# An AdaLN block with a routed FFN on one core: scatters of two sequences read their slot list directly instead of through copied columns

## The chip, the cores and the metric

The kernel runs on one core of a Trainium2 chip. The metric is the time of one execution on the device, in microseconds (us), as the median of several runs. Engines are called as in the profile: PE is TensorE's matmuls, PEld its weight loads, DVE is VectorE, ACT is ScalarE, POOL is GpSimd, and SP is the engine whose queue issues most plain DMAs here. Times inside an execution are those of one profiled execution, counted from the start of its span.

## The reference, cut to what matters

Four sequences of 512 tokens with 128 features pass through one AdaLN block: a convolutional branch, then a mixture of 160 small experts of which each token uses eight, and a shared expert. Both branches are modulated by six vectors per sequence, computed from a condition `c`.

```python
mod = silu(c) @ wmod                              # (4, 6 * 128): sa, ca, ga, sb, cb, gb
ga, gb = sign(ga) * max(|ga|, 0.25), ...          # gates, kept away from zero
h = layernorm(x) * (1 + ca) + sa
# conv branch: rmsnorm, linear 128 -> 512, gate and value,
# two depthwise convolutions, linears, gate, linear 256 -> 128, plus h
x = x + ga * conv_branch(h)
h = layernorm(x) * (1 + cb) + sb                  # called h2 in the kernel
# routed FFN over all 4 * 512 tokens
probs = sigmoid(h @ router_w.T + bias)            # 160 experts
top_w, top_idx = top_k(probs, 8)
top_w = 2.5 * top_w / (sum(top_w) + 1e-9)
h1 = silu(einsum('th,eih->eti', h, w_gate))       # 128 -> 64 for each expert
routed = einsum('eti,ehi->th', h1 * combine.T, w_down)
shared = silu(h @ w_gate_shared.T) @ w_down_shared.T
x = x + gb * (routed + shared)
```

All data are float32. The reference computes every expert for every token; the kernel computes only the chosen ones.

## The kernel before, in words

**Tiles.** A sequence `b` (0 to 3) lies on chip as 128 partitions x 4 token tiles x 128 features. Its work is a generator, `sequence(b)` (lines 286 to 588), which is advanced in stages so that the stages of neighbouring sequences interleave. It computes the modulation, the conv branch (projections L328, convolution taps on PE L370 and on DVE L375), adds `x` (L405), then the second norm and `h2`. Half of `h2` is made by DVE and the other half, two token tiles, by two steps on POOL (a multiplication at L456, an addition at L457). Router probabilities and their top eight follow (DVE, L444 and around), then the ranks of each token within its expert, and at L517 `slot_in`, a list of 4 x 8 unsigned integers per partition: for token tile `t` and choice `k`, the row of a DRAM table in which that token's `h2` is to be put. Near its end the generator runs the shared expert; `wdg` (L569, DVE) and `hs` (L571, ACT) belong to it.

**Scatter.** `dispatch(b)` (lines 632 to 674) puts the 512 rows of `h2` into the table, eight times each. That is 32 indirect DMAs of 128 rows, issued by POOL at L666, each with one column `slot_in[:, t, k]` as its list of rows. Sequences 0 and 1 go into table 0, sequences 2 and 3 into table 1. Some of the scatters do not read the column from `slot_in`; a POOL copy (L664) brings the column into another tile, `pick`, first, and the scatter reads `pick`. In `dispatch(0)` and `dispatch(1)` a copy is made for those 26 of the 32 scatters for which there is no other step to be put in between; the six others have, ahead of them, one of six residual steps (`residual_sums(b + 2)`, L594, L595, L596: `h * gate + x + bias` of sequence `b + 2`, two token tiles at a time), and read `slot_in`. In `dispatch(2)` and `dispatch(3)` every scatter has its copy, and the steps in between are weights of earlier sequences (`places`, L620) and additions of the shared expert's output (L650).

**Experts.** `experts(s)` (lines 681 to 775) works through table `s` in groups of eight blocks. A group loads its rows (`xg`, SP, L690), transposes them on PE (L696), copies them out of PSUM (`xs`, L697, by DVE for s = 0 and by ACT for s = 1), multiplies by the gate weights (L722), applies silu on ACT (L730), multiplies by the down weights (L735) and stores the rows into a result table (ACT's queue, L709). Ten groups have fixed weights; seven more are overflow blocks, for experts with more rows than one block holds. Their weights `ow` are loaded by SP with an address from a register (L749, eight loads a group, two buffers) and used at L759 and L769.

**Combine.** `combine(b)` (lines 778 to 818) fetches, for each token tile and choice, the 128 result rows by an indirect DMA on POOL (L809), 32 for each sequence. For sequences 0 and 1 POOL also multiplies each fetched block by its weight (L786) and DVE adds (L795); for 2 and 3 DVE does both (L791, L793). Sequences 0 and 1 read result 0, sequences 2 and 3 result 1. After the last fetches come the gate and the final addition (L797, L798), and SP stores the output (L985).

**What sets the order.** The main part (lines 961 to 986) emits the stages of the sequences with `dispatch(b - 1)` after them, then `experts(0)`, `combine(0)`, `combine(1)`, `experts(1)`, `combine(2)`, `combine(3)`. That is the order of emission only. A scheduler then decides, when the kernel is built, in which order each engine issues its instructions, from its own estimates of their durations; `behind(b, what)` is a hint to it that an instruction is not to be issued ahead of another. So a removed instruction can also move others. On the chip the order on each engine is fixed, and the engines wait for one another through semaphores.

Some tiles share a buffer by their tag, so that the later one waits until the earlier is read for the last time: `pick` uses the tag of `keys`; `bits` of `places` (L606) that of the modulation `mod` of the sequence two later, which the POOL steps of `h2` read last; `wdg` of sequence 3 (L569) that of `out_bg` of sequence 3, which the last residual step L596 reads; `hs` of sequence 2 (ACT) that of the input `u_f` of the POOL steps of `h2` of sequence 2.

A dense fallback for lists that do not fit (lines 987 on) is guarded by a flag and is not taken with these inputs.

Of the kernel before, what the change touches and what calls it, by code (L numbers as in the profile page):

```python
# [92 lines left out]
def adaln_block(  # L93
# [22 lines left out]
    def own(b, shape, dtype, tag, name):  # L116
        return work.tile(shape, dtype, tag=f"{tag}{b % 2}", name=f"{name}_{b}", bufs=1)
# [165 lines left out]
    def behind(b, what):  # L283
        return tc.issue_after(last[what, b].ins) if (what, b) in last else nullcontext()
# [305 lines left out]
    def residual_sums(b):  # L590
        h, x, mod, out_bg = residual[b]
        for i in range(2):
            at = ds(2 * i, 2)
            yield nc.gpsimd.tensor_mul(h[:, at, :], h[:, at, :], wide(mod[:, 2, :])[:, at, :])  # L594
            yield nc.gpsimd.tensor_add(h[:, at, :], h[:, at, :], x[:, at, :])  # L595
            yield nc.gpsimd.tensor_add(h[:, at, :], h[:, at, :], wide(out_bg)[:, at, :])  # L596
# [35 lines left out]
    def dispatch(b):  # L632


        h2, slot_in = scattered[b]
        pick = own(b, [P, NT, TOPK], U32, "keys", "pick")

        def steps():
            if b < 2:
                for _ in range(11):  # L640
                    yield None
                yield from residual_sums(b + 2)
            else:
                for _ in range(4):
                    yield None
                for other in ((0,), (1, 2))[b - 2]:
                    yield from places(other, nc.gpsimd)
                x1 = x_sb[b]
                for t in range(NT):
                    yield nc.gpsimd.tensor_add(x1[:, t, :], x1[:, t, :], shared[b][:, t, :])  # L650

        between = steps()
        for t in range(NT):
            for k in range(TOPK):
                i = t * TOPK + k
                step = None
                if i and (b >= 2 or i % 2 == 0 or i < 12):
                    with behind(b, "scatter"):
                        step = next(between, None)
                at = slot_in[:, t, k : k + 1]  # L660
                if step is None or b >= 2:
                    at = pick[:, t, k : k + 1]
                    with behind(b, "scatter"):
                        nc.gpsimd.tensor_copy(at, slot_in[:, t, k : k + 1])  # L664
                with behind(b, "scatter") if i else behind(b - 1, "scatter"):
                    last["scatter", b] = nc.gpsimd.indirect_dma_start(  # L666
                        out=tables[b // 2], out_offset=bass.IndirectOffsetOnAxis(ap=at, axis=0),
                        in_=h2[:, t, :], in_offset=None, bounds_check=ROWS - 1, oob_is_err=False,
                    )
                ins = last["scatter", b].ins  # L670
                tc.declare_no_dep(ins, group=f"dispatch{b // 2}", reason="different rows")
                tc.add_to_no_dep_group(f"dispatch{b // 2}", ins)
        for _ in between:
            pass
# [286 lines left out]
    for b in range(B):  # L961
        if 0 < b < 2:
            next(parts[b])
        next(parts[b])
        if b:
            next(parts[b - 1])
        if b == 1:
            with behind(0, "kept"):
                w_pairs = [weights(g) for g in range(NGO - 2)]
        next(parts[b])  # L970
        if 0 < b < B - 1:
            next(parts[b + 1])
        if b:
            dispatch(b - 1)
    next(parts[B - 1])
    dispatch(B - 1)
    for _ in places(B - 1, nc.vector):
        pass
# [79 lines left out]
```

## Time and profile before

| | before |
|---|---|
| three runs | 506.87, 509.65, 512.99 us; median 509.65 |
| profiled execution | 505.33 us, span 503.6 us |
| granted TensorE clock, mean | 0.804 of full speed |
| idle POOL ahead of scatters of `dispatch` (page, group L666) | 34.2 us |
| HBM traffic | 50.54 MB read, 47.45 MB written |

By stage of the span, busy time of each engine in us:

| stretch, us | what runs | PE | DVE | ACT | POOL | clock | DMA share |
|---|---|---|---|---|---|---|---|
| 65 to 121 | scatters of sequence 0 | 49.72 | 42.86 | 25.04 | 46.50 | 0.88 | 0.47 |
| 121 to 177 | scatters of sequence 1 | 36.14 | 31.75 | 18.84 | 47.09 | 0.81 | 0.27 |
| 177 to 299 | experts(0); scatters of 2 and 3 | 91.31 | 55.40 | 37.47 | 83.71 | 0.85 | 0.66 |
| 299 to 411 | experts(1); combine(0), combine(1) | 76.76 | 20.81 | 56.43 | 87.73 | 0.88 | 0.75 |
| 411 to 504 | combine(2), combine(3) | 0.00 | 29.19 | 0.00 | 63.26 | 0.50 | 0.20 |

The clock is the share of full TensorE speed that was granted, and the DMA share is the mean busy share of the core's 16 DMA engines. A POOL instruction that issues an indirect DMA is counted as busy while POOL works on it; the transfer itself goes on after it. A busy share in a table like this says nothing yet on what an engine waits for; that is read from timelines, where each line gives start, duration, engine, source line and operation, and in brackets the idle time before it with what ended it.

### The profile page before, as it was taken

What the parts mean: (1) busy time and instruction counts of PE and PEld (TensorE: products, weight loads), DVE (VectorE), ACT (ScalarE), POOL (GpSimd) and SP (SyncE); (2) the same over time, 40 slices, a digit from 0 to 9 for tenths busy, and PEclk for the clock granted to TensorE, in tenths of its full rate; (3) what the DMA queues carried; (4) which work ended last, traced back from release to release, by engine and by line L of the source; (5) the groups of instructions that cost most, each with busy time, mean ns of one, the idle gap of its engine ahead of it and who ended that gap; (6) DMA issues with size and microseconds to landing.
All of it is one profiled execution on the core that took longest, in us unless ns stands there. A gap on an engine that the chain in (4) does not pass through costs nothing.

```text
span 503.6 us, 6524 instructions
## 1 busy us (share of the span) xinstructions
PE 305.3 (61%) x1892; PEld 223.2 (44%) x1892; DVE 225.5 (45%) x712; ACT 170.7 (34%) x358; POOL 359.7 (71%) x520
## 2 busy tenths in 40 slices
PE   4896996897749659768586665775877910000000
PEld 2654443444323349767575564665766900000000
DVE  7387785795595336574362220201223204333331
ACT  3563636343704227222232131643666610000000
POOL 7716168887888878748877507888889838777771
PEclk9799998699669959889798785995999875555555
DMA  8999996016410246558698566565999832122111
GB/s 262 409 385 409 362 423 259 31 57 179 142 36 32 89 169 205 180 195 278 198 327 267 182 204 209 190 191 181 309 325 348 293 113 63 52 52 73 52 53 38
DMA packets 50364, 98.50 MB, mean 196 GB/s; under 512 B 7633, under 2 KB 26130, under 8 KB 48914
## 3 DMA queue, kind: packets, MB, share of 16 engines
q1 hardware_dynamic: 36144, 61.20, 35.8%
q0 software_dynamic: 8192, 16.79, 11.2%
q10 hardware_dynamic: 5986, 20.03, 10.2%
q8 instruction: 17, 0.28, 0.2%
q14 instruction: 25, 0.20, 0.1%
HBM read 50.54 MB, written 47.45 MB: 195 GB/s over the span
## 4 chain that ended last, share of the span: by engine, by line
PE 37%; POOL 21%; issue 17%; DVE 9%; DMA 8%; ACT 4%; another core or an unknown queue 1%; SPq 1%; ACTq 0%; POOLq 0%; DVEq 0%
POOL yk L809 10%; PE ph L722 7%; POOL table L666 6%; PE py L735 6%; PE px L696 5%; DMA xg<-table 4%; PE pc L370 4%; PE py L769 3%; PE ph L328 3%; PE ph L759 2%; POOL dia L918 1%; DMA result<-yg 1%; PE py L392 1%; DMA ow<-in_w_ov 1%; DMA yk<-result,row 1%
## 5 line engine op out<-in xcount | busy, mean ns | idle before, releaser
L809 POOL DMA_INDIRECT yk<-result,row x128 | 125.2, 978 | 56.1 <-issue 37.0
L666 POOL DMA_INDIRECT table<-h,pick x116 | 118.8, 1024 | 34.2 <-POOL pick L664 17.3
L696 PE MATMUL px<-ident,xg 128*128 128x128 f32 x272 | 43.4, 297 | 26.0 <-DMA xg<-table 22.6
L735 PE MATMUL py<-w_g,h_own 128*128 128x128 f32 x320 | 45.4, 295 | 14.6 <-issue 7.7
L735 PEld LDWEIGHTS py<-w_g,h_own 128*128 128x128 f32 x320 | 41.6, 207 | 16.9 <-ACT h_own L730 8.5
L722 PE MATMUL ph<-xs,w_g 128*128 128x128 f32 x320 | 47.4, 307 | 0.3 <-DVE xs L697 0.3
L696 PEld LDWEIGHTS px<-ident,xg 128*128 128x128 f32 x272 | 33.0, 151 | 31.2 <-DMA xg<-table 22.0
L722 PEld LDWEIGHTS ph<-xs,w_g 128*128 128x128 f32 x320 | 43.9, 219 | 2.7 <-issue 0.7
L793 DVE SCALAR_TENSOR_TENSOR out_sb<-yk,idx,out_sb 128x128 f32<-128x128 f32 x56 | 20.3, 362 | 49.9 <-DMA yk<-result,row 47.2
L697 DVE COPY xs<-px 128x512 f32<-128x512 f32 x34 | 22.8, 685 | 42.9 <-remote 12.4
L795 DVE TENSOR_TENSOR out_sb<-out_sb,yk 128x128 f32<-128x128 f32 x48 | 15.0, 321 | 58.0 <-POOL yk L786 33.7
L730 ACT ACTIVATE h_own<-ph 64x256 f32<-64x256 f32 x80 | 30.3, 379 | 26.3 <-PE px L696 10.2
L707 ACT COPY yg<-py 128x512 f32<-128x512 f32 x34 | 19.9, 586 | 56.4 <-PE px L696 19.3
L664 POOL COPY pick<-slot_in 128x1 uint32<-128x1 uint32 x116 | 25.6, 222 | 17.0 <-DVE slot_in L517 16.5
L769 PE MATMUL py<-ow,h 64*128 64x128 f32 x224 | 19.6, 317 | 22.6 <-issue 15.6
L769 PEld LDWEIGHTS py<-ow,h 64*128 64x128 f32 x224 | 16.6, 216 | 26.6 <-issue 18.0
L370 PE MATMUL pc<-val,dia 128*128 128x512 f32 x64 | 28.1, 592 | 0.0
L786 POOL TENSOR_TENSOR yk<-yk,idx 128x128 f32<-128x128 f32 x64 | 25.8, 412 | 1.0
L375 DVE SCALAR_TENSOR_TENSOR s<-val,vec,s 128x512 f32<-128x512 f32 x32 | 24.9, 778 | 0.6
L697 ACT COPY xs<-px 128x512 f32<-128x512 f32 x34 | 19.3, 588 | 14.9 <-issue 11.8
L328 PE MATMUL ph<-hf,in_wn 128*128 128x512 f32 x32 | 21.3, 806 | 0.8 <-issue 0.7
L708 DVE COPY yg<-py 128x512 f32<-128x512 f32 x17 | 11.7, 687 | 19.2 <-issue 7.9
(249 smaller groups left out, 551.4 us busy)
## 6 DMA issues: line engine op xcount, KB each, us to landing
table<-early SPq DMA_DIRECT2D x2, 8704.0 KB
xg<-table SPq DMA_DIRECT2D x34, 512.0 KB
result<-yg ACTq DMA_DIRECT2D x34, 512.0 KB
ow<-in_w_ov SPq DMA_DIRECT2D x112, 96.0 KB
w_g<-in_w_gd SPq DMA_DIRECT2D x10, 1024.0 KB
yk<-result,row POOLq DMA_INDIRECT x128
table<-h,pick POOLq DMA_INDIRECT x116
x<-in_x SPq DMA_DIRECT2D x4, 256.0 KB
```

Source lines behind the costliest of these rows:

```text
L328: nc.tensor.matmul(ph, in_wn[:, ts(o, P)], hf, start=True, stop=True)
L370: nc.tensor.matmul(pc, dia[:, k, :], val[:, 0, k : k + L], start=(k == 0), stop=(k == npe - 1))
L664: nc.gpsimd.tensor_copy(at, slot_in[:, t, k : k + 1])
L666: last["scatter", b] = nc.gpsimd.indirect_dma_start(out=tables[b // 2], out_offset=bass.IndirectOffsetOnAxis(ap=at, axis=0), in_=h2[:, t, ...
L696: nc.tensor.transpose(px[:, c, :], xg[:, 4 * half + c, :], ident)
L697: (nc.scalar.copy if s else nc.vector.tensor_copy)(xs[:, ds(4 * half, 4), :], px)
L722: nc.tensor.matmul(ph[:, c, :, :].rearrange("u r (i q) -> u r i q", i=8), w[:, j, 0, :], xs[:, :, ds(16 * j, 16)].rearrange("f i (r q) -> ...
L730: nc.scalar.activation(h4[at, :, mine, :], ph4[at, :, mine, :], AF.Silu)
L735: nc.tensor.matmul(py[j & 1][:, j // 2, :], h, w[:, j, 1, :], start=True, stop=True)
L769: nc.tensor.matmul(py[r][:, c, :], h[at, c, :], ow[at, c, r, ds(r * INTER, D)], start=True, stop=True)
L786: last["weight", b] = nc.gpsimd.tensor_mul(row, row, wk[:, t, k : k + 1].to_broadcast([P, D]))
L809: last["fetch", b] = nc.gpsimd.indirect_dma_start(out=yk[:, k, :], out_offset=None, in_=results[b // 2], in_offset=bass.IndirectOffsetOnAx ...
```

## The change

In `dispatch`, the condition under which a column is copied loses its first half. `dispatch(0)` and `dispatch(1)` copy no columns any more, and all of their 64 scatters read `slot_in`; `dispatch(2)` and `dispatch(3)` are as before. 52 POOL instructions fall away. The tile `pick` is still declared for every sequence. Nothing else is edited; the line numbers behind the edit grow by one, because of a blank line. The scheduler orders the changed program anew.

```diff
@@ dispatch(b)
                     with behind(b, "scatter"):
                         step = next(between, None)
                 at = slot_in[:, t, k : k + 1]
-                if step is None or b >= 2:
+                if b >= 2:
                     at = pick[:, t, k : k + 1]
                     with behind(b, "scatter"):
                         nc.gpsimd.tensor_copy(at, slot_in[:, t, k : k + 1])
```

## The prediction

> **What bounds the kernel now.** I read the page's engine table and costliest groups, then the chain of work that ended last, then the timelines of GpSimd (POOL), VectorE (DVE), TensorE (PE) and the SP queue at the places where that chain changes engine, and last the built instruction order of the changed kernel beside the old one. The profiled execution took 505.33 us with a span of 503.6; the median of the three runs is 509.65 (506.87 to 512.99). I sum against the span and add 509.65 - 503.6 = 6.05 at the end.
>
> Engines and groups of the page:
> ```profile
> PE 305.3 (61%) x1892; PEld 223.2 (44%) x1892; DVE 225.5 (45%) x712; ACT 170.7 (34%) x358; POOL 359.7 (71%) x520
> L809 POOL DMA_INDIRECT yk<-result,row x128 | 125.2, 978 | 56.1 <-issue 37.0
> L666 POOL DMA_INDIRECT table<-h,pick x116 | 118.8, 1024 | 34.2 <-POOL pick L664 17.3
> L664 POOL COPY pick<-slot_in 128x1 uint32<-128x1 uint32 x116 | 25.6, 222 | 17.0 <-DVE slot_in L517 16.5
> ```
> POOL is busiest, and nearly all of it is 128 scatters and 128 fetches of about 1 us each. But it is not one chain. The chain that ended last runs on POOL from 138 to 197 us (scatters), on PE from 202 to 404 us (the experts), and on POOL again from 411 to 484 us (fetches). So the change, which touches the scatters at 65 to 176 us, has to pass through two hand-overs before it reaches the end.
>
> The price of a copy, timeline of POOL (start, duration, engine, line; idle before in brackets):
> ```profile
> 118.54 0.98 POOL L666 DMA_INDIRECT table<-h,pick  x1 [0.28 <-issue]
> 119.52 0.19 POOL L664 COPY pick<-slot_in 128x1 uint32<-128x1 uint32 x1
> 119.99 0.98 POOL L666 DMA_INDIRECT table<-h,pick  x1 [0.28 <-issue]
> 121.28 0.97 POOL L666 DMA_INDIRECT table<-h,pick  x1 [0.31 <-issue]
> ```
> With a copy between, scatters start 1.45 us apart; without one 1.29 us apart. The copy's 0.19 us mostly replaces idle time.
>
> First hand-over, POOL to DVE and PE. POOL's last residual step of sequence 3, its last scatter into the first table, and the last step of h2 of sequence 3:
> ```profile
> 159.10 0.74 POOL L596 TENSOR_TENSOR h<-h,out_bg 128x256 f32<-128x256 f32 x1
> 175.05 0.98 POOL L666 DMA_INDIRECT table<-h,pick  x1 [0.28 <-POOL pick L664]
> 196.11 0.72 POOL L457 TENSOR_TENSOR h<-u_f,mod 128x256 f32<-128x256 f32 x1
> ```
> and who waits for them:
> ```profile
> 159.88 0.28 DVE L569 TENSOR_TENSOR wdg<-wds,gb_tok 64x128 f32<-64x128 f32 x1 [5.39 <-POOL h L596]
> 182.76 0.69 DVE L697 COPY xs<-px 128x512 f32<-128x512 f32 x1 [9.33 <-issue]
> 196.86 0.18 DVE L606 TENSOR_SCALAR bits<-row 128x32 uint32<-128x32 uint32 x1 [1.69 <-POOL h L457]
> ```
> ```profile
> 181.60 3.02 PE L696 MATMUL px<-ident,xg 128*128 128x128 f32 x12 [8.91 <-DMA xg<-table]
> ```
> DVE stood 5.39 us for the residual (its buffer goes to wdg of sequence 3), DVE and PE some 9 us for the first table, and DVE 1.69 us for h2 of sequence 3 (its modulation buffer becomes bits of places(1)). Behind that last wait stand DVE's top-8 steps of sequence 3, and behind those PE.
>
> Second hand-over, the start of experts(1), timelines of PE and of the SP queue:
> ```profile
> 297.46 1.16 PE L769 MATMUL py<-ow,h 64*128 64x128 f32 x16 [0.86 <-ACT h L764]
> 308.02 2.91 PE L696 MATMUL px<-ident,xg 128*128 128x128 f32 x12 [9.40 <-DMA xg<-table]
> 310.72 2.99 PE L722 MATMUL ph<-xs,w_g 128*128 128x128 f32 x16
> 313.54 1.13 PE L696 MATMUL px<-ident,xg 128*128 128x128 f32 x8
> ```
> ```profile
> 289.74 13.37 SPq L749 DMA_DIRECT2D ow<-in_w_ov  x16
> 303.21 0.84 SPq L690 DMA_DIRECT2D xg<-table  x2
> ```
> PE idles 9.40 us because SP issues both sets of overflow weights ahead of the first table load, and the second set waits for PE's last matmul of experts(0).
>
> Third, POOL waits for the second result table at the first fetch that reads it:
> ```profile
> 401.74 0.98 POOL L809 DMA_INDIRECT yk<-result,row  x1 [0.16 <-issue]
> 403.31 1.02 POOL L809 DMA_INDIRECT yk<-result,row  x1 [0.16 <-issue]
> 410.98 0.95 POOL L809 DMA_INDIRECT yk<-result,row  x1 [6.64 <-issue]
> ```
> It arrives at 404.6 and stands until 410.98. From there to the end of the span nothing waits but POOL's own queue: 92.6 us. So the end is the time at which that fetch may start, plus all that stands behind it on POOL.
>
> **The change, part by part.** Removed: 52 copies (26 in each of dispatch(0) and dispatch(1); the other 12 scatters read the list already). Nothing is added. The copies were also what the scheduler wove other work around, so its order changes, and three moves matter.
>
> 1. Copies. 52 x 0.166 (1.456 - 1.29) = 8.6 us of POOL. Bounds: nothing, if the scatter itself sets the 1.46 pace in a long row; 0.47 each (copy plus the 0.28 idle behind it), 24 us, if all of it goes. The trace has several bare pairs at 1.29, so I take 0.166. The later 64 fetches without anything between them run at 1.25, so a long bare row is possible on this queue.
>
> 2. Order on POOL before 200 us. The scatters of sequences 0 and 1 now stand as 30, then two residual steps, then 2; the other residual steps follow. Before the last scatter into table 0 four residual steps and one h2 step (0.75 each) are gone too: 8.6 + 3.8 = 12.4, so its end moves from 176.0 to about 163.5. But the last residual step of sequence 3 now stands behind it: five steps of 0.77 and a copy, ready at about 167.5 instead of 159.84. The h2 step of sequence 2 also moves there (146.8 to about 165.7), and ScalarE's hs of sequence 2, which reuses its input buffer, waits with it (154.22 before) with the four copies of low behind it. DVE's wait for the residual grows by 7.7, less one conv tap (0.75) that now stands ahead of it, or 6 to 7. Sequence 3's addition of x, 172.73 before, comes at about 178.7. PE's first transpose of table 0 then starts at once, near 178.7 instead of 181.60: of the 9 us stall, 3 are won, 6 went into a new wait.
>
> Then that lead meets the h2 step of sequence 3. In the old order 11 scatters of sequence 2 stand ahead of its end, in the new order 19. POOL: -8.6 + 8 x 1.456 + one more addition (0.5) = +3.5, or about 200.3 instead of 196.83. Counting the steps one by one with the grouped residual steps at 0.77 gives 199.3. I take +3. DVE, 2.9 early, waits there about 6 us more than before, and everything behind runs 3 us late. The first experts are covered by PE's own work from there; I let the 3 us pass through: experts(0) ends at 301.6 instead of 298.6, and the first fetch of combine starts at 306.7 instead of 303.67. Of SP's queue: the first table loads are issued 12 us earlier, which now costs and brings nothing more than the above. slot_in of sequence 3 comes 3 us late, but POOL stood 4.38 us for it before and still does; its scatters end near 288 instead of 284.9, before table 1 is wanted at 297.
>
> 3. Order on SP at experts(1). The first two loads of table 1 now stand ahead of the second set of overflow weights. First set: issue from 289.74 + 3, 8 of the 16 loads in 4.5 us, so the table load goes at 297.2 and lands 4.77 us later (303.21 to 307.98 before), at 302.1: PE starts 5.9 us earlier than 308.02. The idle shrinks from 9.4 to under 1 us, and the slow matmuls after it go (granted clock 0.5 in that slice): 12 transposes in 2.91 and 16 matmuls in 2.99, against 8 in 1.04 and 16 in 1.95 a little later, 1.3 + 1.0 = 2.4 us. Result 1 may be read at 410.98 - 5.9 - 2.4 = 402.7. Bounds: nothing of the 8.3 (it comes back as waits for later loads, of which the old chain has 4.40 at 332 and 5.93 at 384), all of it.
>
> 4. Order on POOL at the end. The first fetch from result 1 now stands behind 59 fetches and 53 weightings instead of 64 and 58. Fetch and weighting together take 1.57 to 1.61 (401.74 to 403.31; 398.51 to 400.13), so five pairs, 8.05 us, that were done ahead of the wait now stand behind it. POOL arrives at 306.7 + 92.6 = 399.3 and waits until 402.7. The end: 402.7 + 92.6 + 8.05 = 503.4, against 503.6: nothing. With the 6.05 it is 509.4.
>
> A rule that speaks against the change: the Trainium skill, SBUF — State Buffer, "A bandwidth-pool intuition that's wrong", says that GpSimd can't write descriptors while DVE holds the shared port, and gives about 620 ns alone and 3100 ns beside a DVE copy. By it, an estimate, 64 bare scatters beside a busy DVE would cost up to 2.5 us more each, 160 us. The trace decides: beside a DVE that is busy 42.9 of the 56 us from 65 to 121, scatters mostly take 0.98 and the longest of all 1.69, so I add nothing.
>
> **The rivals.** *Slower, by the queue position.* The 8.3 us of move 3 don't reach result 1, because loads and weights of the later groups wait instead. Then result 1 comes at 410.98 + 3 = 414.0 and the end at 414.0 + 92.6 + 8.05 = 514.6, run 520.7. Half of the gain lost gives 507.5, run 513.6. For it: experts(1) has table-load waits right up to 390. Against: their sum is set by PE's release of buffers, which moves with PE. It decides from result 1 at 408 us on (more than 1% slower).
>
> *Faster.* The 3 us of move 2 are absorbed (PE has gaps of 1 to 5 us between 207 and 282 that wait for nothing the profile shows, and a late PE may run into them), and result 1 comes before POOL does. Then only POOL counts: 303.67 + 92.6 + 92.6 + 8.05 = 496.9, run 503.0. For it: POOL would have no wait at all from 304 on. Against: result 1 would have to come by 396.3, 14.7 us earlier.
>
> *The change doesn't do what it says*: the scatters keep 1.46 us. Then move 2 is +11.6 instead of +3, result 1 at 411.3, the end 512.0, run 518.0. The bare pairs at 1.29 speak against it; I count it with slower.
>
> **How the numbers follow.** No change (within 1%, which is about what a measurement of this kernel can tell from no change; 504.6 to 514.7): 0.42. Faster by over 1%: 0.20. Slower by over 1%: 0.38, more than faster, because every microsecond by which result 1 is late counts whole, while gains stop at 497 (503 as a run). Forecast 509.4. The likeliest case alone spans 505 to 514; the range with the rivals, less a tenth at each end, 502 to 520.
>
> **What would show it.** In the changed kernel's profile: bare scatters 1.29 apart with no copy in dispatch(0) and (1) (else step 1 is wrong); last scatter into table 0 near 163 us; DVE's wait for the residual of sequence 3 near 167 and x of sequence 3 near 179; DVE's wait at bits of places(1) of 6 to 8 us, until about 200 (if it ends by 196, move 2 is wrong); PE idle before the first transposes of experts(1) under 2 us and at near full clock (else move 3); POOL idle ahead of the first fetch from result 1 of about 3 us, with five more pairs behind it (if zero, the faster rival; if over 8, the slower one). What would make the forecast wrong is above all the length of PE's two expert stages, whose unexplained gaps (8.05 us at 337) I carried over unchanged.

## The result, and the profile after

The changed kernel took 541.8 us (median of 4 runs, 540.66 to 545.13) against 509.9 us (506.87 to 512.99): a ratio of 1.065, with a 95% interval of 1.060 to 1.070. The profiled execution took 540.71 us with a span of 539.0, 35.4 us more than before. The prediction, 509.4 with a range of 502 to 520, was wrong. Whether the loss appears at all depends on something outside the program, which the experiments show; first its place.

The page of the changed kernel, engines and the groups of the three rows of indirect DMAs:
```profile
PE 301.5 (56%) x1892; PEld 220.5 (41%) x1892; DVE 220.5 (41%) x712; ACT 170.6 (32%) x358; POOL 348.2 (65%) x468
...
L810 POOL DMA_INDIRECT yk<-result,row x128 | 125.1, 977 | 65.0 <-issue 29.3
L667 POOL DMA_INDIRECT table<-h,slot_in x64 | 66.1, 1032 | 40.7 <-issue 18.6
L667 POOL DMA_INDIRECT table<-h,pick x64 | 65.1, 1017 | 19.0 <-POOL pick L665 11.1
```
POOL is busy 11.5 us less (348.2 against 359.7) and the end comes 35 us later: it is no matter of POOL's work. Its timeline in the middle of the first row:
```profile
99.11 0.97 POOL L667 DMA_INDIRECT table<-h,slot_in  x1 [0.30 <-issue]
100.39 0.97 POOL L667 DMA_INDIRECT table<-h,slot_in  x1 [0.30 <-issue]
101.67 0.97 POOL L667 DMA_INDIRECT table<-h,slot_in  x1 [0.30 <-issue]
```
The scatters go at 1.28 us, as forecast. The timeline of DVE beside that row, then beside the second:
```profile
81.82 0.29 DVE L224 SCALAR_TENSOR_TENSOR size<-gb_tok 128x128 f32<-128x128 f32 x1
101.27 0.69 DVE L405 TENSOR_TENSOR x<-po,h 128x512 f32<-128x512 f32 x1 [19.15 <-issue]
...
151.00 0.68 DVE L293 TENSOR_TENSOR u_a<-u_a,mod 128x512 f32<-128x512 f32 x1
175.44 0.69 DVE L405 TENSOR_TENSOR x<-po,h 128x512 f32<-128x512 f32 x1 [23.76 <-remote]
```
and what PE did just before, and what else waited, on ACT:
```profile
79.96 1.83 PE L399 MATMUL po<-out_wg,gate 128*128 128x128 f32 x14 [0.25 <-issue]
145.33 1.95 PE L399 MATMUL po<-out_wg,gate 128*128 128x128 f32 x16
147.12 0.87 PE L232 MATMUL pm<-early 128*128 128x384 f32 x2
```
```profile
111.12 0.58 ACT L308 COPY hf<-px_h 128x512 f32<-128x512 f32 x1 [6.14 <-remote]
149.92 0.48 ACT L234 COPY mod<-pm 128x384 f32<-128x384 f32 x1 [1.89 <-remote]
175.41 0.37 ACT L234 COPY mod<-pm 128x256 f32<-128x256 f32 x1 [25.01 <-remote]
```
The addition of x of sequence 1 (DVE, L405, 101.27) waits for one thing in the built order: the product `po`, whose last matmuls ran at 81.8. It stood 19.15 us after that. The next one stood 23.76 us, with its product done at 147.3 (it waits for POOL's residual too, done at 122.1), and ACT stood 25.01 us for the last product of line 232, started at 147.12. "issue" and "remote" in the brackets say that the profile has no cause for these waits; how late a signal is follows from the end of the matmuls and the start of the reader, not from the bracket. The common part is that each waits for a signal from PE, and that it starts 6 to 28 us after the matmuls were done (a stand, below, is such a wait). SP is slowed as well: its 15 loads of overflow weights, in the timelines of SP's queue before and after:
```profile
116.26 8.93 SPq L749 DMA_DIRECT2D ow<-in_w_ov  x15
```
```profile
140.11 35.16 SPq L750 DMA_DIRECT2D ow<-in_w_ov  x15
```
The kernel before has the same stands, short ones, right behind the place where one scatter follows another with nothing between (the lines at 119.99 and 121.28 above). DVE and ACT there:
```profile
125.33 0.69 DVE L405 TENSOR_TENSOR x<-po,h 128x512 f32<-128x512 f32 x1 [2.78 <-remote]
```
```profile
126.00 0.37 ACT L234 COPY mod<-pm 128x256 f32<-128x256 f32 x1 [4.77 <-remote]
```
I had seen these two and carried them over unchanged, as I did the gaps that the prediction calls unexplained. Those are of the same kind. PE's 5.13 us until 244.18 stand behind ACT's copy of `shared`, 8.1 us after its product, and PE's 8.05 us until 345.80 behind ACT's `h` of line 764, which starts at 345.15, 9.4 us after its product (335.73). PE and ACT, and POOL beside them, in the kernel before:
```profile
233.62 1.16 PE L574 MATMUL psh<-wdg,hs 64*128 64x128 f32 x8
```
```profile
242.87 0.59 ACT L580 COPY shared<-psh 128x512 f32<-128x512 f32 x1 [5.04 <-remote]
```
```profile
232.54 0.98 POOL L666 DMA_INDIRECT table<-h,pick  x1 [0.28 <-issue]
233.83 0.97 POOL L666 DMA_INDIRECT table<-h,pick  x1 [0.30 <-issue]
...
235.27 0.98 POOL L666 DMA_INDIRECT table<-h,pick  x1 [0.28 <-issue]
...
236.73 0.98 POOL L666 DMA_INDIRECT table<-h,pick  x1 [0.28 <-POOL pick L664]
```

How 35.4 us come together, from the timelines of both kernels (start times in us; an L number is that of the kernel before):

| event | before | after | forecast |
|---|---|---|---|
| slot list of sequence 1 (L517) | 107.72 | 131.29 | 107.7 |
| addition of x, sequence 2 (L405) | 125.33 | 175.44 | 125 |
| last scatter into table 0 | 175.05 | 185.32 | 162.5 |
| addition of x, sequence 3 | 172.73 | 220.81 | 178.7 |
| end of PE's experts(0) | 298.62 | 323.47 | 301.6 |
| first transposes of experts(1) | 308.02 | 326.13 | 302.1 |
| first fetch from result 0 | 303.67 | 331.51 | 306.7 |
| first fetch from result 1 | 410.98 | 439.00 | 402.7 |
| last fetch | 492.01 | 528.23 | 491.8 |

The late signals put the work of sequence 2 back by 50 us. Of that, 39.0 are left where PE starts on table 0 (181.60 before, 220.61 after), and 24.9 at the end of experts(0), which takes 102.9 us instead of 117.0. PE's idle time before experts(1) shrinks by 6.7 us, which leaves 18.1; experts(1) then takes 107.5 us instead of 97.5, so result 1 is 28.0 us late; and the five pairs that stand behind it instead of ahead of it add 8.2 us. Behind the last fetch 0.8 us are won.

### The profile page after: what moved, and what is told of

It reads as the page before. It is cut to its first block, busy times and chain, and to the rows that moved or that the text cites. A ratio compares the mean times of both kernels' runs of the same rounds, so it can differ in the third digit from the quotient of the medians.

```text
span 539.0 us, 6436 instructions
## 1 busy us (share of the span) xinstructions
PE 301.5 (56%) x1892; PEld 220.5 (41%) x1892; DVE 220.5 (41%) x712; ACT 170.6 (32%) x358; POOL 348.2 (65%) x468
## 4 chain that ended last, share of the span: by engine, by line
PE 41%; issue 15%; POOL 13%; DVE 8%; DMA 8%; another core or an unknown queue 6%; ACT 5%; SPq 3%; ACTq 1%; POOLq 0%; DVEq 0%
POOL yk L810 11%; PE py L736 6%; PE ph L723 6%; PE px L697 6%; PE pc L370 5%; DMA xg<-table 5%; PE ph L328 3%; PE py L770 3%; SPq L750 2%; PE ph L760 2%; PE py L392 2%; DMA mat<-in_mats 2%; DVE s L375 1%; PE pu L358 1%
## 5 line engine op out<-in xcount | busy, mean ns | idle before, releaser
L667 POOL DMA_INDIRECT table<-h,slot_in x64 | 66.1, 1032 | 40.7 <-issue 18.6
L667 POOL DMA_INDIRECT table<-h,pick x64 | 65.1, 1017 | 19.0 <-POOL pick L665 11.1
L736 PE MATMUL py<-w_g,h_own 128*128 128x128 f32 x320 | 45.0, 295 | 15.9 <-ACT h_own L731 11.5
L697 PE MATMUL px<-ident,xg 128*128 128x128 f32 x272 | 41.1, 286 | 12.5 <-DMA xg<-table 8.2
L723 PE MATMUL ph<-xs,w_g 128*128 128x128 f32 x320 | 45.4, 298 | 2.0 <-issue 1.1
L723 PEld LDWEIGHTS ph<-xs,w_g 128*128 128x128 f32 x320 | 41.8, 209 | 4.6 <-issue 2.3
L697 PEld LDWEIGHTS px<-ident,xg 128*128 128x128 f32 x272 | 31.7, 146 | 17.4 <-issue 8.0
L306 PE MATMUL px_h<-ident,hn 128*128 128x128 f32 x16 | 4.2, 378 | 53.9 <-ACT hn L305 31.7
L770 PE MATMUL py<-ow,h 64*128 64x128 f32 x224 | 18.4, 304 | 18.2 <-ACT h L765 9.7
L375 DVE SCALAR_TENSOR_TENSOR s<-val,vec,s 128x512 f32<-128x512 f32 x32 | 26.9, 841 | 0.6
L306 PEld LDWEIGHTS px_h<-ident,hn 128*128 128x128 f32 x16 | 2.5, 161 | 55.7 <-ACT hn L305 32.5
```

Of the source, the lines that this page charges most:

```text
L375: last["conv", b] = nc.vector.scalar_tensor_tensor(s[:, 1, :], val[:, 1, k : k + L], v("sym_k", KS + k), s[:, 1, :], ALU.mult, ALU.add)
L667: last["scatter", b] = nc.gpsimd.indirect_dma_start(out=tables[b // 2], out_offset=bass.IndirectOffsetOnAxis(ap=at, axis=0), in_=h2[:, t, ...
L697: nc.tensor.transpose(px[:, c, :], xg[:, 4 * half + c, :], ident)
L723: nc.tensor.matmul(ph[:, c, :, :].rearrange("u r (i q) -> u r i q", i=8), w[:, j, 0, :], xs[:, :, ds(16 * j, 16)].rearrange("f i (r q) -> ...
L736: nc.tensor.matmul(py[j & 1][:, j // 2, :], h, w[:, j, 1, :], start=True, stop=True)
L770: nc.tensor.matmul(py[r][:, c, :], h[at, c, :], ow[at, c, r, ds(r * INTER, D)], start=True, stop=True)
```

## The experiments

Theories, in the order in which they came up. 1: a long row of scatters with no other POOL instruction between holds up PE's signals. 2: the transfers do, because they read the list itself. 3: the new order of the residual steps is the cause. 4: the delay belongs to the circumstances of the run and not to the program alone. 5: the pace of the scatters decides. 6: the scatter's wait for its copy decides. Each comparison timed the kernel before anew; its time says which kind of circumstance it met: about 475 us (below: prompt signals) or about 510 us (late signals).

**Runs 1 to 4.** Copies in `dispatch(0)` only (run 1; run 2 has them in `dispatch(1)` only, with b == 1):
```diff
-                if step is None or b >= 2:
+                if (step is None and b == 0) or b >= 2:
```
An unread memset in place of each copy (run 3):
```diff
-                if step is None or b >= 2:
+                if b >= 2:
...
+                elif step is None:
+                    with behind(b, "scatter"):
+                        nc.gpsimd.memset(pick[:, t, k : k + 1], 0)
```
One copy of the whole list before each row (run 4):
```diff
         between = steps()
+        if b < 2:
+            nc.gpsimd.tensor_copy(pick, slot_in)
...
-                if step is None or b >= 2:
+                if b < 2:
+                    at = pick[:, t, k : k + 1]
+                else:
                     at = pick[:, t, k : k + 1]
```


> Copies kept in dispatch(0), none in dispatch(1). Theory 1 (a long row of scatters with no other GpSimd instruction between them keeps TensorE's signals from VectorE, ScalarE and SyncE): the 19 and 6 us stands of sequence 0's row go, slot_in of sequence 1 is back near 108 us, and the 24 us stand of sequence 1's row stays; time some 520 to 532 us. Theory 2 (transfers that read the list itself are the cause): the same here. Theory 3 (the new order of the residual steps is the cause, whichever row it is): the order in dispatch(0) is the old one and that in dispatch(1) the new one, so 520 to 532 us too, but with the loss at the grouped steps and not at VectorE's additions of x.

> No copies in dispatch(0), copies kept in dispatch(1). Theories 1 and 2: the stands beside sequence 0's row stay (slot_in of sequence 1 near 131 us), the 24 us stand beside sequence 1's row shrinks to the 3 us of the kernel before; time some 520 to 532 us. Theory 3: the steps of dispatch(0) alone are grouped, at 107 to 122 us, where little waits for them, so about 510 us.

> Scatters of sequences 0 and 1 all read the list itself, but where the kernel before copied a column a memset of a column that nobody reads stands (the scatter doesn't depend on it). Theory 1: any GpSimd instruction between scatters will do, so about 510 us (505 to 515). Theory 2: the transfers still read the list, so about 540 us.

> One copy of the whole list into pick before each of the first two rows; then the scatters of sequences 0 and 1 read pick, with nothing between them. Theory 1: the row is as bare as in the changed kernel, so about 542 us (535 to 550). Theory 2: no transfer of these rows reads the list itself, so about 510 us.

Measured: 474.8, 475.58, 475.06 and 475.08 us, with the kernel before at 475.9: ratios of 0.998, 1.000, 1.000 and 1.000, all intervals within 0.995 to 1.004. All expectations missed, and so did the ground they stood on: the kernel before itself was 34 us quicker than in the first comparison. In these traces no engine has a wait for PE without a cause, although run 4's scatters are as bare as those of the changed kernel. Theories 1 to 3 can't be the whole story, and theory 4 was formed.

**Run 5: the changed kernel again.**

> The changed kernel itself, unedited, beside the kernel before. If the 32 us that it lost come with the program (theories 1 to 3), it is slower by 6 to 7 per cent again, whatever chip it runs on. If they come with the chip (theory 4: on the chip of the first comparison TensorE's signals to the other engines arrive up to 25 us late while GpSimd scatters, on others they do not), then on a chip where the kernel before takes about 476 us the changed kernel takes 471 to 481 us too, as in the four runs so far, and VectorE's additions of x have no stand of more than 3 us.

547.93 us against 513.44, ratio 1.064 (1.056 to 1.072): this comparison met late signals again. The stands are at the same places and of nearly the same length; DVE's timeline of this run:
```profile
101.07 0.69 DVE L405 TENSOR_TENSOR x<-po,h 128x512 f32<-128x512 f32 x1 [19.93 <-remote]
...
175.24 0.69 DVE L405 TENSOR_TENSOR x<-po,h 128x512 f32<-128x512 f32 x1 [26.72 <-remote]
```
19.93 and 26.72 us against 19.15 and 23.76. So the delay is no accident of one execution.

**Runs 6 and 7** were runs 3 and 4 again:

> The same kernel as in the third run: a memset of a column that nobody reads in place of each removed copy. If the kernel before takes about 476 us here, it tells nothing new (about 475). If it takes about 511 us: theory 1 (any GpSimd instruction between the scatters lets the other engines' signals through) expects 505 to 516 us, SyncE's 15 loads of ow at 0.6 us each and no stand of over 5 us at VectorE's additions of x; theory 2 (reading the list itself is what costs) expects 540 to 550 us.

> The same kernel as in the fourth run: the list copied once, then scatters that read the copy with nothing between them. If the kernel before takes about 476 us here, about 475 again. If it takes about 511 us: theory 1 expects 540 to 550 us with stands of 20 us and more at VectorE's additions of x of sequences 1 and 2; theory 2 expects 505 to 516 us.

They met prompt signals (before 477.27 us; 472.96 and 475.69, ratios 0.991, interval 0.985 to 0.996, and 0.998, 0.995 to 1.002). The 0.991 was not seen in runs 3 and 9 of the same kernel (1.000 and 0.996), so I make nothing of it.

**Runs 8 and 9: the changed kernel, and the memset, once more.**

> The changed kernel, unedited. If the kernel before takes about 511 us here: 540 to 550 us, as twice before. If it takes about 476 us: theory 4 (the loss belongs to chips on which TensorE's signals come late) expects 471 to 481 us, theories 1 to 3 in their plain form expect 6 per cent more than before, some 505 us.

> A memset of a column that nobody reads in place of each removed copy. If the kernel before takes about 476 us here: 472 to 477. If it takes about 511 us: theory 1 (any GpSimd instruction between the scatters will do) expects 505 to 516 us and SyncE's 15 loads of ow within some 10 us; theory 2 (reading the list itself is what costs) expects 540 to 550 us.

Prompt signals: before 475.5 us, changed 474.69, ratio 1.0005 (0.997 to 1.004). Theory 4 holds: where PE's signals are prompt the very same program loses nothing. The memset gave 475.32 (0.996, 0.992 to 1.000).

**Run 11: the kernel before, for its trace with prompt signals.**

> The kernel before, unedited, for its trace. On a chip where it takes about 476 us, theory 4 expects that the waits without a cause in the profile, which took 34 us of the first trace (24 us at L697, 7 us at the additions of x and at mod, 10 us at ScalarE's L764 among them), are all under 2 us, and that copy and scatter still take 1.46 us together. Theories 1 to 3 in their plain form expect the same waits as in the first trace.

474.75 us. The waits without a cause are gone, as expected; the x of sequence 2 no longer waits. (The three groups named there add up to 41 us and not to 34, and the largest wait at L697, 9.33 us until 182.76, was not of this kind: PE started those transposes only at 181.60.) With run 8 this pair shows what the change does when nothing else interferes. POOL, last scatters and first fetches, run 11 and then run 8:
```profile
280.31 0.98 POOL L666 DMA_INDIRECT table<-h,pick  x1 [0.28 <-POOL pick L664]
281.59 1.00 POOL L809 DMA_INDIRECT yk<-result,row  x1 [0.30 <-issue]
282.89 0.96 POOL L809 DMA_INDIRECT yk<-result,row  x1 [0.31 <-issue]
```
```profile
268.62 0.98 POOL L667 DMA_INDIRECT table<-h,pick  x1 [0.28 <-DMA ow<-in_w_ov]
282.07 0.99 POOL L810 DMA_INDIRECT yk<-result,row  x1 [12.47 <-issue]
283.37 0.96 POOL L810 DMA_INDIRECT yk<-result,row  x1 [0.30 <-issue]
```
Without the copies POOL is done with its scatters 11.7 us earlier, and then stands 12.47 us, since result 0 is not there: ACT's last store of it goes out at 276.85, against 274.72 with the copies. The fetches start 0.48 us later than before, and from there POOL has no wait of over 0.8 us until the end in either kernel. So, with prompt signals, the gain is paid back as a wait at the hand-over from experts(0).

**Runs 10, 12 and 13: both questions in one kernel,** the unread memset in `dispatch(0)`, the single copy in `dispatch(1)`:
```diff
         between = steps()
+        if b == 1:
+            nc.gpsimd.tensor_copy(pick, slot_in)
...
-                if step is None or b >= 2:
+                if b >= 2:
...
+                elif step is None and b == 0:
+                    with behind(b, "scatter"):
+                        nc.gpsimd.memset(pick[:, t, k : k + 1], 0)
+                elif b == 1:
+                    at = pick[:, t, k : k + 1]
```


> Two tests in one kernel, to be read row by row: dispatch(0) reads the list itself with an unread memset in place of each removed copy; dispatch(1) copies the whole list once and then scatters from the copy with nothing between. If the kernel before takes about 476 us here, about 475 and no stands. If it takes about 511 us: theory 1 (bare rows) expects no stand of over 5 us at VectorE's addition of x of sequence 1 (beside row 0) and one of over 20 us at that of sequence 2 (beside row 1), with SyncE's 15 loads of ow stretched to over 30 us; theory 2 (reading the list itself) expects the 19 us stand beside row 0 and less than 5 us beside row 1. The time is between 511 and 545 us in both.

> An unread memset in place of each removed copy in dispatch(0), whose scatters read the list itself; one copy of the whole list in dispatch(1), then bare scatters that read the copy. If the kernel before takes about 511 us here: theory 1 (bare rows) expects no stand of over 5 us at VectorE's addition of x of sequence 1, one of over 20 us at that of sequence 2, and SyncE's 15 loads of ow stretched to over 30 us; theory 2 (reading the list itself) the 19 us stand beside row 0 and under 5 us beside row 1. If it takes about 476 us: about 476 and no stands.

Run 10 and its repetition, run 12, met prompt signals: 478.17 and 474.85 us, ratios 1.002 (0.996 to 1.007) and 1.000 (0.997 to 1.003). Run 13 met late ones: 531.24 against 507.82, ratio 1.043 (1.018 to 1.068). Its POOL in the first row, and DVE beside both rows:
```profile
78.45 0.14 POOL L670 MEMSET pick<- 128x1 uint32 x1
78.78 0.97 POOL L674 DMA_INDIRECT table<-h,slot_in  x1 [0.19 <-issue]
79.73 0.13 POOL L670 MEMSET pick<- 128x1 uint32 x1
80.06 0.97 POOL L674 DMA_INDIRECT table<-h,slot_in  x1 [0.19 <-issue]
```
```profile
97.81 0.69 DVE L405 TENSOR_TENSOR x<-po,h 128x512 f32<-128x512 f32 x1 [14.05 <-remote]
...
154.24 0.69 DVE L405 TENSOR_TENSOR x<-po,h 128x512 f32<-128x512 f32 x1 [12.51 <-issue]
```
A POOL instruction between the scatters does not do: the memset fits into the 0.30 us that POOL stands idle anyway, the scatters keep 1.28 us, and DVE still stands 14.05 us. Theory 1 is wrong as stated. Not reading the list does not do either: beside the second row, which reads the copy, DVE stands 12.51 us and ACT 17.23. Theory 2 is wrong as stated, though both stands are shorter than the 19 to 27 us of the changed kernel. SP's 15 loads, beside the second row, took 17.08 us: more than the 9 us with prompt signals, but not over 30 as theory 1 had it. What the two rows share with the changed kernel is the pace.

**Runs 14 to 18: the pace.** `dispatch(0)` reads the list itself, with a memset wide enough to bring the scatters back to the old pace, and no scatter that depends on it; `dispatch(1)` has its copies and such a memset:
```diff
+        idle = work.tile([P, 224], F32, tag="idle", name=f"idle{b}", bufs=1)
...
-                if step is None or b >= 2:
+                if (step is None and b == 1) or b >= 2:
...
+                if step is None and b < 2:
+                    with behind(b, "scatter"):
+                        last["idle", b] = nc.gpsimd.memset(idle, 0.0)
-                with behind(b, "scatter") if i else behind(b - 1, "scatter"):
+                with behind(b, "idle"), behind(b, "scatter") if i else behind(b - 1, "scatter"):
```


> To be read row by row. dispatch(0): the list read directly, and in place of each copy a wider unread memset (128 x 224), so that scatters should start some 1.45 us apart as with copies, without depending on it. dispatch(1): copies as before, and such a memset too (some 1.7 us apart). If the kernel before takes about 510 us here: theory 5 (the pace: scatters 1.28 us apart fill a path that the other engines' signals share, 1.46 apart leave room) expects under 6 us at VectorE's addition of x of sequence 1 (14 us with the narrow memset at 1.28, 19 and 20 bare, none before) and under 1 us at that of sequence 2 (2.8 before); theory 6 (the scatter's wait for the copy is what lets the signals through, not the pace) expects 12 to 20 us beside row 0. If the kernel before takes about 476 us: some 476 to 490 and no stands.

> Last try: dispatch(0) reads the list directly with an unread 128 x 224 memset between (scatters 1.44 us apart); dispatch(1) has the copies and such a memset (1.57 us apart). If the kernel before takes about 510 us here: theory 5 (the pace) expects under 6 us at VectorE's addition of x of sequence 1 and under 1 us at that of sequence 2; theory 6 (the scatter's wait for the copy) expects 12 to 20 us beside row 0. If the kernel before takes about 476 us: 478 to 485 and no stands.

Four of the five met prompt signals: 482.62, 482.11, 481.52 and 481.25 us, 0.9 to 1.7% slower than the kernel before; the best known is the last, 1.009 (1.005 to 1.014). The fifth, run 18, met late ones: 515.22 against 511.18 us, ratio 1.010 (0.996 to 1.024), so like before and not like the changed kernel. POOL, DVE and ACT in run 18:
```profile
72.50 0.97 POOL L671 DMA_INDIRECT table<-h,slot_in  x1 [0.17 <-issue]
73.46 0.30 POOL L669 MEMSET idle<- 128x224 f32 x1
73.93 0.97 POOL L671 DMA_INDIRECT table<-h,slot_in  x1 [0.17 <-issue]
74.89 0.31 POOL L669 MEMSET idle<- 128x224 f32 x1
75.36 0.97 POOL L671 DMA_INDIRECT table<-h,slot_in  x1 [0.17 <-issue]
```
```profile
80.96 0.68 DVE L405 TENSOR_TENSOR x<-po,h 128x512 f32<-128x512 f32 x1
...
124.30 0.69 DVE L405 TENSOR_TENSOR x<-po,h 128x512 f32<-128x512 f32 x1 [1.23 <-remote]
```
```profile
124.34 0.37 ACT L234 COPY mod<-pm 128x256 f32<-128x256 f32 x1 [2.88 <-remote]
```
The scatters start 1.43 us apart, read the list itself, wait for no copy, and the addition of x of sequence 1 does not wait at all (no bracket); SP's 15 loads take 9.34 us. That is theory 5's number, and it speaks against theory 6 (12 to 20 us), on the one trace that there is of this kernel with late signals. Beside the second row, at 1.57 us, DVE stands 1.23 us (theory 5 had said under 1) and ACT 2.88, against 2.78 and 4.77 in the kernel before.

So beside the first two rows PE's signals came up to 28 us late with scatters every 1.28 us, whatever stood between and whatever the transfers read, and only in some circumstances; with scatters every 1.43 to 1.57 us DVE and ACT stood 0 to 5 us there. Further on a slower pace did not keep the signals prompt. ACT's `shared` at 242.87 in the kernel before is 8.1 us late with one bare pair of scatters ahead (232.54 and 233.83) and 1.44 us or more from scatter to scatter after it. ACT's `h` at 270.14 is 3.8 us late with a copy ahead of every scatter from 255 on, and the one at 345.15 is 9.4 us late beside fetches that start 1.25 to 1.6 us apart. So a slower pace went with shorter stands beside the first two rows, and is not shown to be what decides.

What the circumstances are stays open. Late signals were met in 4 of the 13 comparisons (before at 507.8, 509.9, 511.2 and 513.4 us; otherwise 474.1 to 477.3). They aren't tied to a chip's number, as theory 4 first had it: runs 17 and 18 have the same one. The traces differ in one more thing: with late signals they hold 4,491 to 5,004 events of semaphores, with prompt ones 9,091 to 9,216; the kernel before alone has 4,789 and, in run 11, 9,122. Half of these events are missing where signals are late, so the recording may take part in it; all executions here were recorded, so that wasn't tried. Why, at one pace of 1.28, the stand is 14 us in one place and 27 in another is open too, as is theory 3 for what it may add: the order alone was not tried.

## Why the prediction was wrong, step by step

**What failed.** The step that failed is the last sentence of the prediction, "whose unexplained gaps (8.05 us at 337) I carried over unchanged", and in move 2 the times of PE, DVE and ACT from 80 us on, taken as those of the kernel before. The trace that I had was 31.7 us longer than that of the same kernel with prompt signals (503.6 against 471.9 in run 11): it held waits for late signals. In place of the unchanged times the changed kernel showed stands of 19.15 and 23.76 us at DVE and 25.01 at ACT beside the two rows that the change made denser, where the kernel before has 0, 2.78 and 4.77, and result 1 came 28.0 us late. That such waits grow beside denser rows, where signals are late at all, is shown; why they do is open.

**Copies (step 1): right.** 1.276 us bare against 1.29 forecast and 1.456 with a copy. With prompt signals the last scatter into table 0 started 16.2 us earlier (159.98 against 176.15), forecast 12.4.

**Move 2: right in kind, smaller in size, where signals are prompt.** Run 8 against run 11: the residual of sequence 3 is ready 2.8 us later, at 164.5 (forecast 7.7), x of sequence 3 comes 3.7 us later (forecast 6), and PE starts on table 0 1.4 us earlier (forecast 2.9). DVE's wait for h2 of sequence 3 grew by 3.1 us (0.68 to 3.74, forecast 6), but its end moved by 0.2 and not by 3. A wait that I had not priced, DVE at the first `bits`, took 12.08 us; it stands in place of DVE's wait for the residual, 8.68 us in run 11 and none here. The last store of result 0 came 2.1 us later (forecast 3).

**Move 3: right at its start, not at its end.** In the first comparison PE's idle time before experts(1) fell from 9.40 to 2.67 us (forecast under 1); but experts(1) took 10.0 us longer, so none of it reached result 1, which is the bound "nothing of the 8.3". With prompt signals that idle time fell from 12.55 to 0.26 us, and result 1's last store came 5.7 us earlier (372.69 to 366.99; forecast 8.3, in which the 3 us of move 2 are already counted), where nobody waited for it.

**Move 4: right.** From the first fetch of result 1 to the last fetch 81.03 us became 89.23, +8.2 for 8.05 forecast. With late signals these 8 us count whole; with prompt ones POOL never waits there.

**The rule that spoke against the change** (the Trainium skill, SBUF — State Buffer, "A bandwidth-pool intuition that's wrong") has VectorE hold up GpSimd's descriptors, which would make scatters longer. Bare ones mostly took 0.97 us, beside a working VectorE too (from 76 to 81 us of the changed kernel), so it was right to give it no time. What grew longer was the waits of the other engines beside POOL's scatters, ACT and SP among them, and I hadn't asked what a denser row does to others.

**The forecast of no change** fits the one comparison in which the changed kernel met prompt signals (run 8: 1.0005, where 0.9995 was forecast), and in part by luck: the sum let result 1 come 8 us early and the five pairs take it back, while in fact POOL's whole gain stands as a 12.47 us wait for result 0. With late signals POOL stood 15.11 us ahead of the first fetch of result 1, where over 8 was the prediction's sign for the *slower rival*. That rival has the right last part (late result 1, plus 92.6, plus 8.05) with the wrong cause, and puts result 1 at 414.0 where it was read at 439.00.

## What to carry to other kernels

A wait for which the profile names no cause is an unknown that the change may move: find what it waits for and when that was done, and ask what could make it longer before carrying it over, above all if the change makes some engine's row denser. An instruction that seems only to cost time between DMAs also sets their pace. And time the kernel before anew beside each run: here it moved by some 7%, as much as the change made it differ, and the verdict with it.

## What the runs showed of the hardware that was not expected

- In the comparisons with late signals, beside indirect DMAs issued every 1.28 us: signals from PE up to 28 us late, and SP's 15 loads at 2.3 us each (1.1 in run 13) instead of 0.6. In run 18, at 1.43 us, DVE's addition of x beside the first row does not wait, and SP's loads take 0.6 us. At 1.44 us and more, behind one bare pair, a signal in the kernel before is still 8.1 us late. In the other comparisons none of this occurs, at 1.28 us either.
- The same program at 475 and at 510 us, the changed one at 475 and at 542 to 548, with no difference inside the program.
- A memset of 128 x 1 between scatters costs nothing (1.28 us with and without); one of 128 x 224, 0.30 us, brings them to 1.43 to 1.44.
